# A four-layer convolution network on one core: the MLP's two halves formed together, the closing 1x1's loads issued one chunk later, the input loaded ahead of the weights

## The chip, the core and the metric

The kernel runs on one core of a Trainium2 chip. The metric is the device time of one execution in microseconds; the change is judged by the median of several executions. Before the change it is 3634.83 us (three runs, 3633.97 to 3635.65). All times within the kernel come from one profiled execution and are counted from the start of its span.

## What is computed

The input x is (3, 256, 48, 48), float32. Four layers follow each other, each of the form x = x + layer(groupnorm(x)), with 32 groups. All the edits lie in the first layer, an attention block; cut to what matters, it is this (B = 3, CC = 128, NB = 2):

```
y = silu(batchnorm(conv1x1(x, cv1_w)))          # 256 -> 256 channels
y1, y2 = y[:, :128], y[:, 128:]
outs, cur = [y1, y2], y2
for i in range(2):
    # the three batch entries serve as q, k and v of the attention
    cur = cur + attention(groupnorm1(cur), qkv_w[i], proj_w[i])
    h2 = groupnorm1(cur)
    f = gelu(conv1x1(h2, f1_w[i], f1_b[i]))     # 128 -> 256 channels
    cur = cur + conv1x1(f, f2_w[i], f2_b[i])    # 256 -> 128 channels
    outs.append(cur)
out = silu(batchnorm(conv1x1(concat(outs), cv2_w)))   # 512 -> 256 channels
```

Layer 1 is a 3x3 convolution whose weights are mixed, per batch entry, from eight expert kernels (`routing`, a sigmoid, then a weighted sum); layer 2 is a plain 3x3 convolution; layer 3 is a selective-scan block.

## The kernel before

Channels lie on the 128 partitions and the 2304 pixels along the free dimension, cut into NCH = 6 chunks of CH = 384. The engines are named as in the profile: PE multiplies, ACT (ScalarE) evaluates functions, DVE (VectorE) and POOL (GpSimd) do elementwise work, SP issues most loads, and ACT's queue issues some. Each engine takes its instructions in order, a load's issue included. The batch entries are worked on in the order 2, 1, 0 (`ORDER`).

The program goes through these stages.

1. **The start.** SP issues the small vectors (L118, L148), then the weights of layer 0 in two parts (`w0a` L375, 640 KB; `w0b` L377, 1024 KB), the attention's projection `pj` (L379, 128 KB), and then, per batch entry, x in two loads of 1152 KB, one for each 128 channels (L407). The statistics of the group norm run on DVE, one instruction for each chunk (L178) and an aggregate (L181); a chain of small steps over PE, DVE and POOL (L184 to L193, L160, L162, L410) turns them into a scale for the weights (L414) and a bias (L419 to L425). The 1x1 convolution (L431) needs all of these, and `w0a`. It has 48 PE records for a batch entry; silu (L435) reads its results. Its outputs go to DRAM (`ycat`, L439, L440), and `cur` also stays in SBUF.
2. **The first attention**, from about 100 to 724 us. Its order is written out by hand; `keep_order` ties each instruction to the one before it on its engine.
3. **The MLP between the attentions** (L805 to L823). For each batch entry and chunk `hidden` forms the 256 inner channels: for each half m, a matmul (L485) into its half of a PSUM pair, then gelu on ACT (L489). `add_back` multiplies back (L495) and DVE adds to `cur` (L499). Each chunk's `add_back` is called after the next chunk's `hidden`. The pair of PSUM comes from a pool with three buffers here (`pss`). This stage is ordered by a scheduler, which also moves work of the next attention between (`vt` L783, norms, `mlp_weights`).
4. **The second attention**, to about 1410 us.
5. **The last MLP and the closing 1x1**, from about 1410 to 1610 us, again in the written order (L882 to L930). For each batch entry six chunks of `hidden` and `add_back` are followed by six chunks of `concatenated`: sixteen PE records over the concatenated channels (L866), silu on ACT (L871), and POOL's addition of x (L876). The concatenated channels that were stored come back through `parts`, which issues two loads for a chunk on ACT's queue: `yc` (L855, 576 KB, read by PE) and `xc` (L857, 384 KB, read by POOL). Both have three buffers (`ypool`). Three chunks are loaded ahead of the loop; then, after chunk c, ACT issues the loads of the chunk three further on (L914). The pairs come from a pool with two buffers (`pss2`). Between the chunks, `aside` advances other work by a step: the norm and the routing of the batch entry finished before (L184, L193, L352, L353, L357), and the mixing of the expert kernels of batch entry 2 (48 pieces of 384 KB, `wconv`, issued by SP at L249 into six buffers; the first six are scaled on ACT at L273, the others added on DVE at L275), two steps after an MLP chunk and three after a chunk of the 1x1. After chunk 3 of batch entry 0, DVE forms the first input tile of the coming convolution (L324 to L335) and finishes the mixed weights (L256 to L261).
6. **The 3x3 convolutions** (L1348) begin at 1627.77 us, and layers 2 and 3 follow to the end of the span.

The whole network is built twice in the program; the second, a more careful attention, runs only when a flag is set, and the profile shows none of it.

Of the kernel before, what the change touches and what calls it, by code (L numbers as in the profile page):

```python
# [16 lines left out]
P = 128  # L17
B = 3
HW = 48
N = HW * HW  # L20
# [6 lines left out]
NCH = N // CH  # L27
# [42 lines left out]
W0_SPLIT = W0_AT["f1"]  # L70


ORDER = (2, 1, 0)
# [10 lines left out]
def net(  # L84
# [21 lines left out]
    nc = tc.nc  # L106
# [98 lines left out]
    def norm_stats(*args):  # L205
        return at_once(norm_steps(*args))
# [15 lines left out]
    def chunk(t, c):  # L222
        return t[:, c * CH : (c + 1) * CH]
# [136 lines left out]
    with ExitStack() as l0:  # L360
# [11 lines left out]
        mean1 = wpool.tile([P, P], F32, name="mean1")  # L372
        nc.gpsimd.memset(mean1, 1.0 / P)
        w0a = epool.tile([P, W0_SPLIT], F32, name="w0a")
        nc.sync.dma_start(w0a, w0[:, :W0_SPLIT])  # L375
        w0b = wpool.tile([P, NW0 - W0_SPLIT], F32, name="w0b")
        nc.sync.dma_start(w0b, w0[:, W0_SPLIT:])  # L377
        pj = epool.tile([P, NB, P], F32, name="pj")
        nc.sync.dma_start(pj, projw.rearrange("i p o -> p i o"))  # L379

        def w(name, at, n):
            a = W0_AT[name] + at
            if a < W0_SPLIT:
                return w0a[:, a : a + n]
            return w0b[:, a - W0_SPLIT : a - W0_SPLIT + n]
# [14 lines left out]
        with ExitStack() as p1:  # L400
            xin = p1.enter_context(tc.tile_pool(name="xin", bufs=2))
            y1p = p1.enter_context(tc.tile_pool(name="y1p", bufs=2))
            ps = p1.enter_context(tc.tile_pool(name="ps0", bufs=5, space=PSUM))
            for b in ORDER:
                xb = xin.tile([P, CT, N], F32, name="xb")
                for ct in range(CT):
                    nc.sync.dma_start(xb[:, ct, :], x[b, ct * P : (ct + 1) * P, :])  # L407
                _, gm, rstd = norm_stats([xb[:, ct, :] for ct in range(CT)], gmat, ps, "s")
                sh = small.tile([P, CT], F32, name="gsh", bufs=4)
                nc.vector.scalar_tensor_tensor(sh, gm, -1.0, rstd, ALU.mult, ALU.mult)  # L410
                ws = y1p.tile([P, CT, 256], F32, name="cv1s", bufs=2)
                pb = ps.tile([P, 512], F32, tag="s", name="ps_b1")
                for ct in range(CT):
                    nc.vector.tensor_scalar(  # L414
                        ws[:, ct, :], w("cv1", ct * 256, 256), rstd[:, ct : ct + 1], None, ALU.mult
                    )
                for m in range(2):
                    for ct in range(CT):
                        nc.tensor.matmul(  # L419
                            pb[:, m : m + 1], w("cv1", ct * 256 + m * P, P), sh[:, ct : ct + 1],  # L420
                            start=ct == 0, stop=ct == CT - 1,
                        )
                bb = small.tile([P, 2], F32, name="bb")
                nc.vector.tensor_tensor(bb, pb[:, :2], b1sc, ALU.mult)
                nc.vector.tensor_tensor(bb, bb, b1sh, ALU.add)  # L425
                y1 = y1p.tile([P, N], F32, name="y1")
                for c in range(NCH):
                    for m, dst in ((0, y1), (1, cur[b])):
                        pm = ps.tile([P, 512], F32, tag="s", name="ps_y")
                        for ct in range(CT):  # L430
                            nc.tensor.matmul(  # L431
                                pm[:, :CH], ws[:, ct, m * P : (m + 1) * P], chunk(xb[:, ct, :], c),
                                start=ct == 0, stop=ct == CT - 1,
                            )
                        nc.scalar.activation(  # L435
                            chunk(dst, c), pm[:, :CH], AF.Silu,
                            bias=bb[:, m : m + 1], scale=b1sc[:, m : m + 1],
                        )
                nc.sync.dma_start(ycat[b][:, 0, :], y1)  # L439
                nc.sync.dma_start(ycat[b][:, 1, :], cur[b])  # L440
# [6 lines left out]
        def pair():  # L447
            return pss.tile([P, 2, 512], F32, tag="s", name="ps_s")
# [31 lines left out]
        def hidden(b, c):  # L480
            wf, fb = mlp[b]
            f = fpool.tile([P, 2, CH], F32, name="f")
            pf = pair()
            for m in range(2):
                nc.tensor.matmul(  # L485
                    pf[:, m, :CH], wf[:, m * P : (m + 1) * P], chunk(cur[b], c),
                    start=True, stop=True,
                )
                nc.scalar.activation(f[:, m, :], pf[:, m, :CH], AF.Gelu, bias=fb[:, m : m + 1])  # L489
            return f  # L490

        def add_back(i, b, c, f):
            pf = psa.tile([P, 512], F32, name="acc")
            for m in range(2):
                nc.tensor.matmul(  # L495
                    pf[:, :CH], w("f2", (i * 2 + m) * P, P), f[:, m, :], start=m == 0, stop=m == 1
                )
            cc = chunk(cur[b], c)
            nc.vector.scalar_tensor_tensor(cc, pf[:, :CH], v("f2_b", i), cc, ALU.add, ALU.add)  # L499
# [352 lines left out]
        def parts(b, c):  # L852

            yc = ypool.tile([P, 3, CH], F32, name="yc")
            nc.scalar.dma_start(yc, ycat[b][:, :, c * CH : (c + 1) * CH])  # L855
            xc = ypool.tile([P, CT, CH], F32, name="xc")
            nc.scalar.dma_start(  # L857
                xc, x[b, :, c * CH : (c + 1) * CH].rearrange("(t p) n -> p t n", p=P)
            )
            return yc, xc  # L860

        def concatenated(b, c, yc, xc):
            pz = pair()
            for m in range(2):
                for kt in range(4):
                    nc.tensor.matmul(  # L866
                        pz[:, m, :CH], w("cv2", kt * 256 + m * P, P),
                        yc[:, kt, :] if kt < 3 else chunk(cur[b], c), start=kt == 0, stop=kt == 3,
                    )
            for m in range(2):  # L870
                nc.scalar.activation(  # L871
                    chunk(xs[b][:, m, :], c), pz[:, m, :CH], AF.Silu,
                    bias=b2sh[:, m : m + 1], scale=b2sc[:, m : m + 1],
                )
            both = xs[b][:, :, c * CH : (c + 1) * CH]
            nc.gpsimd.tensor_tensor(both, both, xc, ALU.add)  # L876

        def take_stats(b, c, stats):
            for m in range(2):
                nc.vector.bn_stats(stats[m][:, c, :], chunk(xs[b][:, m, :], c))  # L880

        i = NB - 1  # L882
        mark = listed[-1]
        chunks = [(b, c) for b in ORDER for c in range(NCH)]
# [4 lines left out]
        def aside(n):  # L889

            if small_steps:
                try:
                    next(small_steps[0])
                except StopIteration:
                    del small_steps[0]
            if 2 in route:
                for _ in range(n):
                    next(mixing, None)

        for n, b in enumerate(ORDER):  # L900
            held = None
            for c in range(NCH):
                f = hidden(b, c)
                if held is not None:
                    add_back(i, *held)
                held = b, c, f
                aside(2)
            add_back(i, *held)
            stats = [
                small.tile([P, NCH, 6], F32, name=f"xst{m}", bufs=2) for m in range(CT)  # L910
            ]
            for c in range(NCH):
                concatenated(b, c, *ahead.pop(0))
                z = n * NCH + c + 3  # L914
                if z < len(chunks):
                    ahead.append(parts(*chunks[z]))
                if c:
                    take_stats(b, c - 1, stats)
                if b == 0 and c == 3:
                    vp = late_pool("vp", 2, last_pools)  # L920
                    pad = late_pool("pad", stack=last_pools)
                    first_v = input_transform(2, 0, *norms[2])
                aside(3)
            take_stats(b, NCH - 1, stats)
            if b:
                curpools[b].close()
            small_steps.append(routing(b, psm, "m", stats))
# [10 lines left out]
    rooms, w3v, chunks = {}, {}, {}  # L938
# [399 lines left out]
    with ExitStack() as l1:  # L1338
# [95 lines left out]
        for n, (k, h) in enumerate(halves):  # L1434
            layer, b = units[k]
# [36 lines left out]
    with ExitStack() as l3:  # L1472
# [134 lines left out]
        for s, (at, m, h) in enumerate(steps):  # L1607
            if m == 0 and h == 1 and at + 2 <= last:
                fetch(at + 2)
            for part in range(8):  # L1610
                j = 4 * m + 2 * h + part // 4
# [150 lines left out]
```

## Time and profile before

| what | us |
|---|---|
| median of three runs | 3634.83 |
| lowest and highest | 3633.97, 3635.65 |
| the profiled execution | 3635.14 |
| its span | 3633.4 |
| busy: PE, DVE, ACT, POOL | 3195.8, 3007.2, 2338.1, 1442.2 |
| mean granted clock of PE | 0.929 of full |

The profiled execution is 1.7 us longer than its span and 0.3 us longer than the median of the runs. The page of a profile gives the busy time of each engine and, for groups of instructions, how long one takes and what the engine waited for before it. The timeline lists instructions in order of time; a line reads start, duration, engine, line of the source, operation, output <- inputs, and in brackets the idle time before it with what ended it. A 128x384 matmul in float32 shows as two PE records. "ACTq" and "SPq" mark what the queue of ACT or SP issues. A view by windows gives the busy time of each engine in stretches that one names. A wait is put down to the event that came last, so the engine named is not always the cause.

### The profile page before, as it was taken

To read this page: it belongs to the slowest core of one execution; us is meant where nothing else is said; L and a number is where in the kernel's file an instruction comes from. 1 tells how busy PE (TensorE), PEld (TensorE's weight loads), DVE (VectorE), ACT (ScalarE), POOL (GpSimd) and SP (SyncE) were. 2 spreads that over 40 slices of the span, in tenths; PEclk is the share of its full clock that TensorE was granted. 3 is DMA by queue.
4 is the path that set the end of the run, shared out by engine and by line. 5 is a ranking of instruction groups with operands and counts; after the bars stand their busy time and mean duration, and the time that the engine had idled before them with its cause. 6 is when DMAs were issued, how large, how long until landed. Compare 5 with 4: busy or idle time off the path is not lost. (4 is left out here: it accounts for less than half of the span.)

```text
span 3633.4 us, 45544 instructions
## 1 busy us (share of the span) xinstructions
PE 3195.8 (88%) x17154; PEld 1441.3 (40%) x17154; DVE 3007.2 (83%) x3304; ACT 2338.1 (64%) x3477; POOL 1442.2 (40%) x386
## 2 busy tenths in 40 slices
PE   6999999999999998867899988888888888888875
PEld 4323232342322324436677753333333333333331
DVE  3798989959989895369966469999999999999996
ACT  2688777748877875332123347777777777777774
POOL 0000000000000000210000039999999999999997
PEclk9999999999999999978899998988899999888886
DMA  4000000000000001656502134444444444444441
GB/s 171 11 1 1 1 2 1 1 39 1 2 1 1 2 1 66 198 180 220 184 15 57 46 85 103 115 109 106 107 114 96 110 101 107 111 113 101 111 105 36
DMA packets 169209, 266.50 MB, mean 73 GB/s; under 512 B 42689, under 2 KB 135937, under 8 KB 166802
## 3 DMA queue, kind: packets, MB, share of 16 engines
q1 hardware_dynamic: 150642, 243.44, 25.0%
q10 hardware_dynamic: 18336, 20.06, 1.8%
q8 instruction: 136, 2.23, 0.3%
q14 instruction: 95, 0.78, 0.1%
HBM read 216.31 MB, written 46.89 MB: 72 GB/s over the span
## 5 line engine op out<-in xcount | busy, mean ns | idle before, releaser
L603 ACT ACTIVATE pt<-ps_s 128x1024 f32<-128x1024 f32 x972 | 938.9, 1022 | 237.0 <-PE ps_s L599 219.2
L1564 DVE TENSOR_TENSOR_SCAN hs<-ps_da,hs 128x385 f32<-128x385 f32 x1152 | 1012.7, 939 | 61.1 <-ACT ps_da L1556 43.2
L679 DVE TENSOR_TENSOR part<-part,pt 128x2048 f32<-128x2048 f32 x396 | 906.7, 2290 | 80.9 <-ACT pt L603 56.4
L1556 ACT ACTIVATE ps_da<-dtr,u 128x384 f32<-128x384 f32 x1152 | 658.2, 582 | 311.0 <-DVE hs L1564 292.6
L162 POOL TENSOR_TENSOR rstd<-ve,mhalf 128x2 f32<-128x2 f32 (+1 forms) x26 | 17.9, 690 | 1564.4 <-DVE ve L160 1564.4
L599 PE MATMUL ps_s<-q,kt 32*128 32x512 f32 (+1 forms) x4320 | 616.3, 594 | 2.3 <-DVE q L560 0.9
L612 PE MATMUL acc<-pt,vt 128*32 128x512 f32 (+1 forms) x4320 | 522.9, 563 | 8.2 <-DVE o L659 8.0
L1348 PE MATMUL ps_c<-vt,u 128*128 128x288 f32 x1728 | 432.1, 412 | 44.4 <-DVE u L261 30.2
L1572 POOL TENSOR_TENSOR hc<-hs,x 128x3072 f32<-128x3072 f32 x72 | 445.9, 6193 | 36.7 <-PE ps_g L1147 13.4
L1572 POOL TENSOR_TENSOR hc<-hs,bc 128x3072 f32<-128x3072 f32 x72 | 443.8, 6165 | 37.2 <-PE ps_g L1147 13.6
L1101 PE MATMUL ps_g<-u 128*128 128x384 f32 x1152 | 388.3, 492 | 3.1 <-ACT u L1110 3.1
L1348 PEld LDWEIGHTS ps_c<-vt,u 128*128 128x128 f32 x1728 | 331.6, 193 | 139.5 <-issue 33.4
L599 PEld LDWEIGHTS ps_s<-q,kt 32*128 32x128 f32 x4320 | 220.1, 183 | 389.2 <-issue 228.5
L1101 PEld LDWEIGHTS ps_g<-u 128*128 128x128 f32 x1152 | 214.6, 190 | 174.1 <-issue 13.3
L1589 PE MATMUL ps_y<-hc,u 128*32 128x384 f32 x2304 | 247.5, 553 | 29.8 <-POOL hc L1572 26.5
L1531 POOL TENSOR_TENSOR hs<-dtur,x 128x1536 f32<-128x1536 f32 x72 | 248.3, 3449 | 16.2 <-DMA dtur<-dtud 12.8
L1531 POOL TENSOR_TENSOR hs<-dtur,bc 128x1536 f32<-128x1536 f32 x72 | 248.2, 3447 | 6.9 <-DMA dtur<-dtud 4.3
L612 PEld LDWEIGHTS acc<-pt,vt 128*32 128x32 f32 x4320 | 95.7, 108 | 365.4 <-issue 329.5
L1147 PE MATMUL ps_g<-wconv,u 17*128 17x384 f32 x144 | 79.2, 684 | 97.2 <-ACT x L1168 97.2
L1364 ACT COPY cb<-ps_c 128x288 f32<-128x288 f32 x48 | 19.1, 397 | 221.6 <-PE ps_c L1348 203.4
L1589 PEld LDWEIGHTS ps_y<-hc,u 128*32 128x32 f32 x2304 | 64.6, 118 | 200.5 <-issue 148.0
L1059 PE MATMUL ps_g<-wconv,u 128*128 128x384 f32 x144 | 86.6, 773 | 65.3 <-ACT x L1168 64.9
(236 smaller groups left out, 3548.4 us busy)
## 6 DMA issues: line engine op xcount, KB each, us to landing
wconv<-in_we SPq DMA_DIRECT2D x144, 384.0 KB, 4.3
dtr<-dtd SPq DMA_DIRECT2D x288, 192.0 KB, 3.9
dtur<-dtud SPq DMA_DIRECT2D x288, 96.0 KB, 4.1
wconv<-xd SPq DMA_DIRECT2D x36, 384.0 KB, 4.5
x<-bcd SPq DMA_DIRECT2D x72, 192.0 KB, 5.6
dtd<-x SPq DMA_DIRECT2D x36, 384.0 KB, 2.4
bc<-bcd SPq DMA_DIRECT2D x72, 192.0 KB, 5.4
yc<-ycat ACTq DMA_DIRECT2D x18, 576.0 KB, 4.9
```

Of the source, the lines that this page charges most:

```text
L599: nc.tensor.matmul(s[:, j, cols], kt[r, mt * P : (mt + 1) * P], q[r, :n], start=True, stop=True,)
L603: nc.scalar.activation(p[:, h0 : h0 + 2, :], s, AF.Exp)
L612: nc.tensor.matmul(acc[h * HD : (h + 1) * HD, :n], vt[:, mt, g * P + h * HD : g * P + (h + 1) * HD], p[:, h, cols], start=mt == 0, stop=mt ...
L679: nc.vector.tensor_tensor(part, first_p if group == 1 else part, p, ALU.add)
L1059: nc.tensor.matmul(bank[to], w3v["less"][:, int(to != ct), :], k.xg[:, ct, :], start=ct == 0, stop=ct == CT - 1,)
L1101: nc.tensor.matmul(bank[m % 2], w3v["wtap"][:, tap, ct, m * P : (m + 1) * P], k.xn[:, ct, tap : tap + CH], start=tap == 0 and ct == 0, sto ...
L1348: nc.tensor.matmul(pc[:, :HN], u[:, i, dy, ct, m * P : (m + 1) * P], vt[:, i, ct, dy * TW : dy * TW + HN], start=ct == 0 and dy == 0, stop ...
L1531: nc.gpsimd.tensor_tensor(hs[:, :, 2:4, 1:], k.rows[m][1].unsqueeze(1).broadcast_to([P, 2, 2, CH]), bb, ALU.mult,)
L1556: nc.scalar.activation(slots[n % 3][:, 1 : CH + 1], chunks[at].rows[m][0][:, q, :], AF.Exp, scale=amat[:, col : col + 1],)
L1564: nc.vector.tensor_tensor_scan(b, slots[(8 * s + part) % 3][:, : CH + 1], b, 0.0, ALU.mult, ALU.add)
L1572: nc.gpsimd.tensor_tensor(hc, tiles[s][:, :, :, 1:], cb.broadcast_to([P, 2, 4, CH]), ALU.mult)
L1589: nc.tensor.matmul(k.y_ps[32 * q : 32 * q + 32, :CH], fold, hc[:, g, q, :], start=False, stop=h == 1 and g == 1,)
```

## The change

Three edits, all in layer 0.

- In the start, the loads of x come first in SP's queue. The first batch entry's x is split into twelve loads, six for each 128 channels, of one chunk each. `w0a` is issued after them, `pj` and `w0b` after the x of the second batch entry.
- In `hidden`, both matmuls are written ahead of the two gelus. This touches the MLP between the attentions and the last MLP.
- In the closing 1x1, the loads issued after chunk c are those of the chunk two further on instead of three. Three chunks are still loaded ahead of the loop, so nothing is issued after the first chunk.

```diff
@@ layer 0, start
         w0a = epool.tile([P, W0_SPLIT], F32, name="w0a")
-        nc.sync.dma_start(w0a, w0[:, :W0_SPLIT])
         w0b = wpool.tile([P, NW0 - W0_SPLIT], F32, name="w0b")
-        nc.sync.dma_start(w0b, w0[:, W0_SPLIT:])
         pj = epool.tile([P, NB, P], F32, name="pj")
-        nc.sync.dma_start(pj, projw.rearrange("i p o -> p i o"))
...
             for b in ORDER:
                 xb = xin.tile([P, CT, N], F32, name="xb")
+
+                parts = 6 if b == ORDER[0] else 1
                 for ct in range(CT):
-                    nc.sync.dma_start(xb[:, ct, :], x[b, ct * P : (ct + 1) * P, :])
+                    for j in range(parts):
+                        at = slice(j * N // parts, (j + 1) * N // parts)
+                        nc.sync.dma_start(xb[:, ct, at], x[b, ct * P : (ct + 1) * P, at])
+                if b == ORDER[0]:
+                    nc.sync.dma_start(w0a, w0[:, :W0_SPLIT])
+                if b == ORDER[1]:
+                    nc.sync.dma_start(pj, projw.rearrange("i p o -> p i o"))
+                    nc.sync.dma_start(w0b, w0[:, W0_SPLIT:])
@@ hidden
                     start=True, stop=True,
                 )
+            for m in range(2):
                 nc.scalar.activation(f[:, m, :], pf[:, m, :CH], AF.Gelu, bias=fb[:, m : m + 1])
             return f
@@ the closing 1x1
             for c in range(NCH):
                 concatenated(b, c, *ahead.pop(0))
-                z = n * NCH + c + 3
-                if z < len(chunks):
+
+                z = n * NCH + c + 2
+                if 3 <= z < len(chunks):
                     ahead.append(parts(*chunks[z]))
```

## The prediction

> **What bounds the kernel now.** The page first, its busy times:
>
> ```profile
> PE 3195.8 (88%) x17154; PEld 1441.3 (40%) x17154; DVE 3007.2 (83%) x3304; ACT 2338.1 (64%) x3477; POOL 1442.2 (40%) x386
> ```
>
> TensorE (PE) and DVE are busy most of the span, but in different stages, and the chain that ended last names only the last 12 us, so the value of each edit is read from its own stage. I asked for busy time by stages, with borders taken from the timeline: the start up to the first convolution, the MLP between the attentions, then for batches 2, 1 and 0 the last MLP and the closing 1x1 in turn, and the wait after them. The columns are window, length, then busy us of PE, weight loads, DVE, ACT and POOL, the granted clock, the DMA engines' share, GB/s.
>
> ```profile
> 0.00:24.30 24.30, 2.90 (x13) 2.76 (x13) 10.32 (x34) 1.28 (x1) 4.11 (x17) 1.00 0.72 281
> 724.60:784.00 59.40, 58.36 (x189) 32.66 (x188) 31.84 (x79) 22.90 (x39) 1.62 (x3) 1.00 0.10 40
> 1410.30:1444.10 33.80, 22.27 (x62) 11.51 (x61) 8.85 (x27) 10.34 (x16) 0.54 (x1) 0.80 0.46 158
> 1444.10:1475.10 31.00, 31.00 (x98) 18.27 (x97) 5.72 (x11) 6.17 (x10) 9.04 (x5) 1.00 0.54 151
> 1475.10:1511.20 36.10, 23.88 (x58) 12.23 (x57) 6.26 (x22) 17.45 (x25) 2.50 (x2) 0.76 0.25 79
> 1511.20:1542.10 30.90, 30.90 (x97) 18.21 (x96) 22.43 (x26) 7.29 (x11) 10.26 (x5) 1.00 0.94 331
> 1542.10:1578.80 36.70, 25.06 (x58) 12.39 (x57) 20.21 (x37) 13.52 (x19) 2.77 (x2) 0.77 0.58 203
> 1578.80:1609.90 31.10, 31.10 (x97) 18.04 (x95) 19.57 (x25) 8.72 (x12) 11.05 (x8) 1.00 0.64 210
> ```
>
> PE is full in each 1x1 (31.0 of 31.0), and a third idle, with its clock down to 0.76 to 0.80, in each last MLP. The start is a wait for loads: engines are all but idle, the DMA engines 0.72 busy, and DVE's first statistic runs at 12.19:
>
> ```profile
> 12.19 2.86 DVE L178 BATCH_NORM_STATS2 bnst<-xb 128x6 f32<-128x384 f32 x6 [7.26 <-DMA xb<-in_x]
> ...
> 18.14 0.32 DVE L181 BATCH_NORM_AGGREGATE mv<-bnst 128x2 f32<-128x36 f32 x1
> ```
>
> The ACT and PE timelines at the border of batch 1 show why the MLP is slow:
>
> ```profile
> 1475.27 0.53 ACTq L855 DMA_DIRECT2D yc<-ycat  x1
> 1475.84 0.66 ACT L871 ACTIVATE x<-ps_s,cv2sh,cv2sc 128x384 f32<-128x384 f32 x1
> 1478.41 0.37 ACTq L857 DMA_DIRECT2D xc<-in_x  x1
> 1478.81 1.28 ACT L489 ACT_TABLE_LOAD   x1 [2.31 <-POOL x L876]
> 1480.11 0.58 ACT L489 ACTIVATE f<-ps_s,fb 128x384 f32<-128x384 f32 x1
> ```
> ```profile
> 1475.07 0.81 PE L485 MATMUL ps_s<-cur,wf 128*128 128x384 f32 x2
> 1480.74 2.92 PE L485 MATMUL ps_s<-cur,wf 128*128 128x384 f32 x4 [4.87 <-ACT f L489]
> 1484.40 1.65 PE L485 MATMUL ps_s<-cur,wf 128*128 128x384 f32 x2 [0.73 <-ACT f L489]
> 1485.84 2.77 PE L495 MATMUL acc<-f,w0b 128*128 128x384 f32 x4
> ```
>
> The xc load at L857 refills a buffer that POOL's add of this very chunk still reads; ACT issues in order, so the table load and the first gelu queue behind it. The second half's matmul waits until gelu has read the first half, though it writes other columns. After 4.9 us of idling PE works at half speed: the four records of one return product took 2.77 us (a logical matmul is two records), where at full clock the next group starts 1.29 us later (744.62 to 745.91), 0.322 a record.
>
> **What the Trainium skill says.** "TensorE: Matmul & The Clock Gate", Part 1: PE runs at half clock after an idle window of about 3.4 us until about as long a busy one. The trace agrees (2.77 against 1.29 us). "ScalarE: Activation LUTs", What ACT_TABLE_LOAD costs: about 1283 ns for a load; here 1.28. "DMA: Bandwidth & Descriptors", Issuing engines are not separate DMA queues: loads from ACT and SP share the same engines. It agrees: yc landed in 4.1 us in batch 2's 1x1, in 4.7 to 8.5 in the others, beside SP's wconv loads.
>
> **Part 1, the input ahead of the weights.** Before, w0a, w0b and pj (1792 KB) pass through SP's queue before x; the second half's aggregate ends at 18.14 + 0.32 = 18.46. Now SP issues twelve parts of 192 KB from 1.71 on, some 0.45 us each (L375 to L379). I put the first landing at 4.0 (vec: 58 KB in 1.8 us, and 0.5 for the larger size at 420 GB/s), then one part each 0.58 us, a little more than issue (0.45) or bytes (0.47), as their rows are short: the last at 10.4. One statistic (0.55) and the aggregate (0.32): 11.3, a gain of 7.2. Batch 1's statistics, two of which (0.55 each) sat between L188 and L190, now stand behind the chain: 0.3 more. From the seventh part on an issue also waits for the load eight before it (the instruction order shows it), with w0a and batch 1's x queued behind on SP; eight parts in flight are 3.7 us of bytes at 420 GB/s against 2.3 to land, so that is no brake. Together 7.5; bounds 5.5 (parts at 0.75 us) and 9.5 (paced by issue alone). What moves: w0a, behind all parts, lands near 12.3, needed at L414 about 14.9; batch 1's x lands near 17, its convolution starts near 38; vb, w0b and pj are needed after 85 us; POOL's queue is not touched. All cost nothing. The convolution of batch 2, and what follows, starts at 16.8 for 24.3.
>
> **Part 2, both halves first, between the attentions.** Period per chunk there: 2.93 us (741.69 to 744.62), work 8 records of 0.322 = 2.58. So 0.35 lost in about 10 of 18 chunks, as the others already had two halves together, and 0.5 at the start: 4. Bounds 2 and 6. Gelu of the first half now waits for both matmuls, 0.65 later: only the chunk's second gelu stands behind it, and the return product comes after the next chunk's pair, so it is hidden; without that pair between, it would cost 0.65 a chunk. Batch norms and vt keep PE busy after it.
>
> **Parts 2 and 3 in the last MLPs.** Let h be a pair of hidden matmuls (1.29), a the return product (1.29), f two gelus (1.05).
>
> Batch 2: ACT still issues three chunk loads until 1417.5, so gelu starts at 1418.85 as before; but two h are ready. PE order after: h0 h1 a0 h2 a1 ... a5. f0 is done at 1419.9; a0 and part of h2 run at half clock (PE was idle since 1413.5), to 1424.7; then eight of 1.29 and 0.8 of small products: 1436.0. Before: 1444.1. Gain 8.
>
> Batch 1, from t = 0 at h0: silus end 1.4, the loads' buffer was freed a chunk ago, table 1.45 to 2.73, f0 3.8 (before: first gelu at 5.0, a0 at 10.8). a0 3.9, then gm, h2, a1, gv, h3, a2: 10.7. The routing chain remains: L499 to sigmoid took 2.05 us, so sigmoid at 12.95; two L273 (1.76) and a table load: f4 17.3, two L273, f5 20.2, a5 21.6. Before 36.1. Gain 14.5; less 1.5, if one idle window halves the clock: 13.
>
> Batch 0: the same, but DVE does two L275 (1.94) between the steps of the norm chain, which becomes the limit: aggregate 5.5, gd 8.9, pooled 13.0, sigmoid 17.0, then h4 at half clock after 4 us of idling, table, f4, f5, a5 near 26. Before 36.7. Gain 10.7.
>
> The cost is part 3's own: yc for chunk c+2 is issued at the end of chunk c, so it must land in 5.16 - 0.2 = 5.0 us, where it had 10. Cover is one chunk of PE work. In batch 2 it lands in 4.1: free. In batches 1 and 0, with landings 4.7, 4.9, 5.3, 7.7 and about 5.5, 8.5 for the six loads that count, the excess sums to 0.3 + 2.7 + 0.5 + 3.5 = 7; a stall also slows DVE and so SP's competing loads, so I take 5, bounds 0 and 15. If xc is late it stops POOL and the statistics behind it, not PE, and it has a chunk more. The first product of a chunk reads yc, so a late load holds all of PE's queue. Lost cover would cost the whole landing, 4.1 us or more a chunk.
>
> After chunk 3 of batch 0 DVE's own chain (L324 to L261, 1603.5 to 1627.5) sets when the next convolution may start; it hangs on POOL's add of that chunk, so all of it moves. Last stage: 8 + 13 + 10.7 - 5 = 26.7, bounds 12 and 35.
>
> **The sum.** 7.5 + 4 + 26.7 = 38.2 off the profiled execution (span 3633.4 and 1.7 around it, 3635.1), which stands 0.3 above the median of 3634.8: 3597.
>
> **The rivals.** (a) The norm chain and ACT's tables fill most of the gap: for it stands that sigmoid still waits for four engines and that DVE stands in L275; against it that PE's largest waits (4.87, 5.19) go. Last stage 12: 3611. (b) The clock stays full and no yc is late: 38.2 + 5 + 1.5 + 3 (batch 0's h4): 3587. (c) The end of the stage is set by the 48 mixing steps and their 19 MB: only parts 1 and 2 count, 11.5: 3623. Against: DVE idles 4.22 us before L324, and 42 more loads of 0.39 MB with 12 chunks of 0.98 MB, 28 MB in some 89 us, need 318 GB/s, where 331 was reached. (d) Slower: the yc loads at L855, queued in the ring with six wconv loads, land so late that each of the six tight chunks stalls. It takes 43.2 us of stalls to eat the gain, 7.2 each, that is landings over 12.2; the longest seen is 8.5. At 13.5 us, 8.5 each, 51: 3643. (e) That the halves stay apart is excluded by the instruction order, in which each pair stands together with no wait between.
>
> **Chances.** Forecast 0.57 (own range 3590 to 3606), (a) 0.20, (b) 0.13, (c) 0.07, (d) 0.03. The range 3581 to 3614 takes in the forecast, (a) and (b), so 0.9 before misjudged sizes. A measurement can tell about 0.2%, 7.3 us, from no change: faster 0.96, same 0.01, slower 0.03.
>
> **What would show it.** First L178 near 4, first long convolution near 16.8; MLP period 2.6; the three last MLPs at 26, 22 and 26 us with clock above 0.8; PE waits on yc of 0 to 3 us in the 1x1 of batches 1 and 0. Yc landings over 8 us, or the wait before L1348 much above 17.9, would prove me wrong.

## The result, and the profile after

The kernel after took 3597.6 us (median of 4 runs, 3594.8 to 3598.5) beside 3635.2 for the kernel before (median of 4 runs, the three of the table above and one more): a ratio of 0.9895, 95% interval 0.9878 to 0.9913. All ratios below are likewise to the kernel before, run beside the kernel in question. The forecast was 3597. The profiled execution after spans 3596.3 us, 37.1 less than before. Lines of the code up to L374 keep their numbers; in the parts at issue they move by 6 to 8 (the hidden matmul L485 is now L491, gelu L496, return product L502, the 1x1's matmul L873, yc's load L862, xc's L864, and the first matmul of the 3x3 convolutions L1356). That matmul is the first to use the mixed weights and is called the first mixing matmul below; "the mixing starts" means its start.

The busy times by stage, in the columns of the table before (window, length, PE, weight loads, DVE, ACT, POOL, granted clock, DMA share, GB/s):

```profile
0.00:18.43 18.43, 2.88 (x13) 2.74 (x13) 8.78 (x30) 1.28 (x1) 4.11 (x17) 1.00 0.86 298
718.70:776.00 57.30, 56.72 (x193) 33.93 (x193) 32.87 (x84) 20.92 (x39) 1.62 (x3) 1.00 0.15 62
1401.55:1427.17 25.62, 19.47 (x62) 11.65 (x61) 8.85 (x27) 9.53 (x16) 0.54 (x1) 0.87 0.60 208
1427.17:1458.13 30.96, 30.96 (x97) 18.24 (x96) 5.72 (x11) 6.20 (x11) 9.04 (x5) 1.00 0.41 128
1458.13:1478.88 20.75, 17.98 (x57) 9.58 (x56) 6.26 (x22) 15.73 (x24) 2.51 (x2) 1.00 0.34 109
1478.88:1515.85 36.97, 33.14 (x97) 18.83 (x96) 20.40 (x27) 8.13 (x12) 9.69 (x5) 0.95 0.92 322
1515.85:1539.82 23.97, 19.47 (x57) 10.52 (x56) 17.66 (x36) 12.71 (x19) 2.83 (x2) 0.93 0.70 231
1539.82:1572.60 32.78, 30.86 (x96) 17.88 (x95) 17.88 (x23) 8.88 (x13) 10.06 (x8) 1.00 0.74 246
```

Read the third, fifth and seventh row, the last MLPs: 25.6, 20.75 and 24.0 us for 33.8, 36.1 and 36.7. Two things shrank. In batch 1, PE's idle time fell from 12.2 to 2.8 us, and the same matmuls took 17.98 us of PE in place of 23.88, because the clock stayed at 1.00. The sixth and eighth row show the price: two of the three 1x1s, which PE filled in 30.9 to 31.1 us, now take 37.0 and 32.8.

The border of batch 1 in the timeline, ACT and PE together:

```profile
1458.13 3.04 PE L491 MATMUL ps_s<-cur,wf 128*128 128x384 f32 x8
...
1458.96 0.57 ACTq L864 DMA_DIRECT2D xc<-in_x  x1
...
1459.67 1.28 ACT L496 ACT_TABLE_LOAD   x1
1460.96 2.00 ACT L496 ACTIVATE f<-ps_s,fb 128x384 f32<-128x384 f32 x4
...
1461.59 1.56 PE L502 MATMUL acc<-f,w0b 128*128 128x384 f32 x4 [0.42 <-ACT f L496]
```

Four halves (8 records) stand together without a wait; xc is issued 0.83 after the MLP's start where it was 3.34, as its buffer is free; the table load follows at 1.54 (before 3.74), and PE waits 0.42 us where it waited 4.87.

One of the stalls that pay for it, in batch 1's 1x1:

```profile
1495.53 0.55 ACTq L862 DMA_DIRECT2D yc<-ycat  x1
...
1503.76 3.67 PE L873 MATMUL ps_s<-yc,w0b 128*128 128x384 f32 x6 [3.17 <-DMA yc<-ycat]
```

The load issued at 1495.53 lands 8.1 us later. PE waits 3.17 us for it, and then takes 3.67 us for six records that take 2.10 at full clock.

The start, DVE and PE:

```profile
4.53 1.10 DVE L178 BATCH_NORM_STATS2 bnst<-xb 128x6 f32<-128x384 f32 x2 [1.59 <-DMA xb<-in_x]
6.70 0.56 DVE L178 BATCH_NORM_STATS2 bnst<-xb 128x6 f32<-128x384 f32 x1 [1.07 <-DMA xb<-in_x]
...
12.97 0.32 DVE L181 BATCH_NORM_AGGREGATE mv<-bnst 128x2 f32<-128x36 f32 x1
...
18.43 0.99 PE L437 MATMUL ps_y<-xb,cv1s 128*128 128x384 f32 x1
```

The first statistic runs at 4.53 in place of 12.19, and the long convolution starts at 18.43 in place of 24.27, 5.84 earlier.

Where the 37.1 us of span lie: the start 5.84; nothing up to the first MLP (700.2 us of convolution and attention for 700.3); 2.8 from there to the last stage; 26.67 between the last stage's first hidden matmul and the first mixing matmul (190.79 for 217.46); 1.66 in the two milliseconds behind it, which the change doesn't touch and which vary by up to 4.1 among the kernels below (2003.5 to 2007.6).

### The profile page after: what moved, and what is told of

Its sections match the earlier page's. It is cut to its first block, busy times and chain, and to the rows that moved or that the text cites. A ratio compares the mean times of both kernels' runs of the same rounds, so it can differ in the third digit from the quotient of the medians.

```text
span 3596.3 us, 45582 instructions
## 1 busy us (share of the span) xinstructions
PE 3179.0 (88%) x17154; PEld 1438.0 (40%) x17154; DVE 3003.0 (84%) x3304; ACT 2333.6 (65%) x3477; POOL 1440.4 (40%) x386
## 3 DMA queue, kind: packets, MB, share of 16 engines
q1 hardware_dynamic: 152082, 243.44, 25.2%
## 5 line engine op out<-in xcount | busy, mean ns | idle before, releaser
L1356 PE MATMUL ps_c<-vt,u 128*128 128x288 f32 x1728 | 430.0, 410 | 45.7 <-DVE u L261 45.7
L1356 PEld LDWEIGHTS ps_c<-vt,u 128*128 128x128 f32 x1728 | 330.3, 192 | 140.1 <-issue 34.8
```

The lines of the kernel that those rows point to most:

```text
L1356: nc.tensor.matmul(pc[:, :HN], u[:, i, dy, ct, m * P : (m + 1) * P], vt[:, i, ct, dy * TW : dy * TW + HN], start=ct == 0 and dy == 0, stop ...
```

## The experiments

Each kernel is named with its edit. The table, worked out from the timelines' first matmuls, carries most of what follows: start of the first long convolution, start of the last stage, then the lengths of MLP and 1x1 in turn (the last column of these ends with the first mixing matmul), when that matmul starts, and the median.

| kernel | conv. at | stage at | MLP 2 | 1x1 | MLP 1 | 1x1 | MLP 0 | 1x1 to mixing | mixing at | median |
|---|---|---|---|---|---|---|---|---|---|---|
| before | 24.27 | 1410.3 | 33.8 | 30.96 | 36.1 | 30.96 | 36.7 | 48.99 | 1627.8 | 3635.2 |
| after | 18.43 | 1401.6 | 25.6 | 30.96 | 20.75 | 36.97 | 24.0 | 52.51 | 1592.3 | 3597.6 |
| input alone | 18.18 | 1404.3 | 33.6 | 30.96 | 36.05 | 30.96 | 36.5 | 48.98 | 1621.4 | 3627.8 |
| halves alone | 24.44 | 1407.5 | 25.8 | 30.96 | 23.05 | 30.96 | 26.2 | 48.98 | 1593.4 | 3602.8 |
| later loads alone | 24.20 | 1411.2 | 33.9 | 30.96 | 32.8 | 36.5 | 30.2 | 51.2 | 1626.9 | 3632.4 |
| input and halves | 17.94 | 1400.5 | 25.0 | 30.96 | 22.9 | 30.96 | 29.1 | 48.98 | 1588.3 | 3594.5 |
| yc three ahead, xc two | 18.56 | 1401.3 | 25.7 | 30.96 | 20.76 | 30.96 | 26.9 | 48.98 | 1585.5 | 3587.3 |
| both one ahead | 18.67 | 1402.0 | 25.9 | 52.5 | 20.75 | 68.1 | 25.0 | 70.3 | 1664.6 | 3670.0 |
| less mixing in MLP 0 | 18.79 | 1401.0 | 25.2 | 30.96 | 20.75 | 30.96 | 25.5 | 51.8 | 1586.1 | 3590.2 |
| loads after the MLP | 17.96 | 1400.5 | 25.4 | 30.96 | 20.75 | 30.96 | 25.7 | 48.97 | 1583.2 | 3589.5 |
| both of these | 17.61 | 1399.5 | 24.9 | 30.96 | 20.76 | 30.96 | 22.1 | 51.8 | 1581.0 | 3589.9 |

Each row is one execution, and stretches with the same code do not repeat exactly, so the table also says what can be told apart. Among the eight kernels with the new start the convolution begins at 17.61 to 18.79. In all rows with the halves batch 2's MLP has the same code, and it takes 24.9 to 25.9 us (26.7 in a kernel of the last experiment). A 1x1 in which PE never waits repeats within 0.02 us. Batch 0's MLP repeats worst: the two kernels with the halves and without the later loads have the same code there and take 26.2 and 29.1. A difference of one or two microseconds in it shows nothing by itself.

### Each part alone

The first three kernels are the kernel before with one of the three parts of the change's diff each; the fourth is the kernel after without the last part. They have no diff of their own.

Input alone:

> The kernel before with the input ahead of the weights and nothing else. Theory (the start's gain is kept to the end, as every later stage begins from it): the trace of the kernel after starts the first long convolution 5.84 us earlier, so 3635.2 - 5.8 = 3629.4, bounds 3628 and 3631. Rival (a later wait for a load or for GpSimd absorbs it): 3635.

Measured: 3627.8, ratio 0.9977 (0.9969 to 0.9986). The start gained 6.1 in its trace and the mixing began 6.3 earlier, so nothing absorbs it: the rival's 3635 is out. The median lies just below the theory's bound of 3628. Its gain of 7.7 is 1.4 more than the stages account for, no more than the stretch behind the mixing varies.

Halves alone:

> The kernel before with both hidden halves formed first and nothing else. Theory (the halves alone restore most of the last MLPs; the blocked ACT costs some 2.3 us and one half-clock window in each of batches 1 and 0): 2.9 between the attentions, 8.2 in batch 2's MLP, about 11.6 in batch 1's, about 10 in batch 0's, no stall on yc: 32.7 off, 3602.5, bounds 3598 and 3608. Rival (without the later loads the MLPs of batches 1 and 0 stay near 33 us, as ScalarE's late table load is what lets TensorE fall to half clock): 2.9 + 8.2 + 6, 3618.

Measured: 3602.8, ratio 0.9913 (0.9899 to 0.9926). The theory's 3602.5 holds, and 3618 is out. The one added line in `hidden` brings the mixing's start 34.4 us forward: 2.8 between the attentions, 8.0, 13.0 and 10.5 in the three last MLPs, where 2.9, 8.2, 11.6 and 10 were forecast. The blocked table load is still there, and costs little:

```profile
1467.57 0.38 ACTq L858 DMA_DIRECT2D xc<-in_x  x1
...
1468.03 1.28 ACT L490 ACT_TABLE_LOAD   x1 [2.37 <-POOL x L877]
```

xc is issued when POOL's add has ended, 3.35 us into the MLP, the table load waits 2.37 us for that, and batch 1's MLP is 2.3 longer than in the kernel after.

Later loads alone:

> The kernel before with the last 1x1 loads one chunk later and nothing else. Theory (the earlier gelu leaves TensorE idle for 2.6 us instead of 4.9, so that it may keep its clock, and the 1x1 loses about 8 to late yc): MLPs of batches 1 and 0 shorter by 6 to 9 each, so 3635.2 - 15 + 8 + 1 = 3629, bounds 3625 and 3640. Rival (only together with the halves: split halves keep TensorE at half clock): MLPs 2.3 shorter each, 1x1 8 longer, 3638.

Measured: 3632.4, ratio 0.9987 (0.9978 to 0.9995), between the two theories and nearer to the first's 3629. The MLPs of batches 1 and 0 gain 3.3 and 6.5, the two 1x1s lose 5.6 and 2.2, and the mixing starts 0.9 earlier. The first theory's reason, that a pause of 2.6 us lets TensorE keep its clock, holds in one MLP and fails in the other. In batch 1 the pause was 2.57 us and half clock followed at once; in batch 0 it was 2.66 us and the clock stayed full until the routing, 16 us later. Over the whole MLPs the clock was 0.79 and 0.89. The windows that tell the two pauses apart stand in the last section.

Input and halves, the later loads left out:

> The kernel after with the last 1x1 loads put back, issued three chunks ahead. Theory (in company of the other two parts the later loads give about what their stalls take: some 3.7 us in batch 1's MLP and 2.7 in batch 0's against 6.0 and 2 in the 1x1): 3597, within 4 of the kernel after's 3597.6. Rival (the later loads carry the MLPs' gain): 3612. Other rival (the stalls are worse than the blocked ScalarE): 3590 or less.

Measured: 3594.5, ratio 0.9889 (0.9874 to 0.9904), beside 0.9878 to 0.9913 for the kernel after: they can't be told apart, as the first theory had it. By the stages, the later loads give 2.2 in batch 1's MLP and 5.1 in batch 0's, and take 6.0 and 3.5 behind them: 2.3 lost. With the halves alone batch 0's MLP took 26.2 and not 29.1; against that the loads give it only 2.2, and more is lost. The code of the two is the same there, but one had two windows of 3.41 us at half clock in it and the other four. The third part of the change is worth nothing on its own balance; the first two carry it all (7.7 and 32.7 alone, 41.0 together).

### What the later loads cost, and how to keep their gain

Both loads one chunk ahead, the cover taken away wholly:

```diff
-                z = n * NCH + c + 2
+                z = n * NCH + c + 1
```

> The kernel after with the last 1x1 loads one chunk ahead in place of two: the suspected cost, cover of yc, is taken away wholly for 13 of 18 chunks. Theory (TensorE then stalls in each for the whole landing, 4.1 us in batch 2 and about 5.5 in the others, and computes the next products at half clock, 2.2 more): 3 x 6.3 + 10 x 7.7 less the 9.5 already paid, so about 87 later, 3684, bounds 3655 and 3700. Rival (a stall only gives the mixing on DVE time that it needs anyway, so the end of the stage hardly moves): 3610 or less.

Measured: 3670.0, ratio 1.0095 (1.0079 to 1.0112). The mixing starts 72 later than in the kernel after, where 87 was expected. What waited for yc, and the time from issue to landing, from the view of that tile:

```profile
  DMA yc<-ycat: 75.3, 15
...
DMA to landing us min/median/max: 4.2/4.4/5.9
```

Thirteen of these waits are of PE's matmuls, 4.4 to 6.1 us each, 62 in all. In batch 2's 1x1 three stalls cost 21.5 and in batch 1's five cost 37.1, on average 7.2 and 7.4 each: the stall, and some 2.5 us for products at half clock behind it. In batch 0 five stalls cost only 21.3, three times 7.1. The missing 14 us are the two stalls behind chunk 3, hidden beside DVE's chain to the mixing, as the prediction read that stage: from ScalarE's instruction that opens this chain (L310) to the mixing 25.7 us passed here, and 27.2 in the kernel after, which has no stall there. The rival, that stalls cost next to nothing, is out.

yc three chunks ahead as before the change, xc two as after it, in place of `parts`, which loads both:

```diff
+                z = n * NCH + c + 3
+                if z < len(chunks):
+                    ahead.append(part_y(*chunks[z]))
+                if 3 <= z - 1 < len(chunks):
+                    ahead_x.append(part_x(*chunks[z - 1]))
```

> The kernel after with the two last 1x1 loads taken apart: yc three chunks ahead as before the change, xc two chunks ahead as after it. Theory (only xc's buffer blocks ScalarE, as GpSimd's add still reads it, and only yc's short cover stalls TensorE): MLPs stay at 20.8 and 24.0 us, batch 1's 1x1 returns to 30.96 (6.0 off) and batch 0's stretch to the mixing to 49.0 (3.5 off): 3597.6 - 9.5 = 3588, bounds 3585 and 3591. Rival (the stalls are the transfers' bandwidth, not their issue time): 3597. Rival (xc with two chunks' cover holds GpSimd's add and through it the routing): 3593.

Measured: 3587.3, ratio 0.9867 (0.9851 to 0.9884), the lowest median here; its runs (3585.4 to 3590.8) all lie below those of the kernel after. From the view of yc's tile:

```profile
L875 PE MATMUL ps_s<-yc,w0b x216: 486/486/486, 1427.0 to 1566.5; 128*128 128x384 f32 x108
...
DMA to landing us min/median/max: 4.1/6.0/9.9
```

All 216 matmuls that read yc take the same 486 ns, and none waits, though the landings became longer (median 6.0, in the kernel after 4.7). So the transfers' bandwidth was not the stall; their issue time was. The other rival, that xc comes late for POOL, is out too. All 18 additions waited for ScalarE's silu and none for xc; what their engine waited for, from the view of xc's tile:

```profile
  ACT x L880: 98.9, 18
```

yc's buffer is freed by PE's own read of the chunk and blocks nobody; only xc's, which POOL's add still reads, held ScalarE. Both 1x1s return to 30.96 and 48.98. But batch 0's MLP took 26.9, not 24.0. The table load came 4.8 us after its start, where it came 1.6 in the kernel after:

```profile
1512.50 0.53 ACTq L861 DMA_DIRECT2D yc<-ycat  x1
1514.01 0.40 ACTq L866 DMA_DIRECT2D xc<-in_x  x1
1514.52 1.28 ACT L496 ACT_TABLE_LOAD   x1 [3.40 <-DVE u L275]
```

The silus ended at 1511.13, and yc's issue stood until 1512.50, xc's until 1514.01, with the table load behind both; xc's buffer was free. A semaphore is the counter that tells of a load's landing. In the trace this yc load has the semaphore of the wconv load that SP issued at 1505.45 and that landed at 1512.48, and this xc load that of the wconv load of 1506.38, which landed at 1513.95. Each issue came within 0.06 us of that landing: ScalarE waited for transfers of another queue that had been under way for 7.0 and 7.6 us.

Two edits on top of that kernel. Less mixing in batch 0's MLP, more behind it:

```diff
-                aside(2)
+                aside(2 if b else 1)
...
-                aside(3)
+                aside(3 if b else 4)
```

> The kernel with yc three chunks ahead and xc two (3587.3), with one mixing step in place of two per chunk of batch 0's last MLP, and four in place of three per chunk of the 1x1 behind it. Theory (DVE's L275 between the steps of the norm chain is what makes batch 0's MLP longer than batch 1's 20.8): the chain has three pairs of L275 in it, 0.97 off each, so the MLP falls from 26.9 to about 24, the 1x1 has room for one more step a chunk (4 x 0.95 + 1.0 = 4.8 of 5.16 us), total 3584.4. Rival (the MLP waits for ScalarE's blocked loads, not for DVE): MLP 26.5, 3587. Other rival (the moved steps come late behind the 1x1): 3590.

The two loads that stand ahead of the table load issued after the MLP:

```diff
+            if n:
+                load(n * NCH + 2)
...
+                if c < NCH - 1:
+                    load(n * NCH + c + 3)
```

> The kernel with yc three chunks ahead and xc two (3587.3), with the two loads that stand between a batch's last silu and the next MLP's first gelu issued after that MLP instead. Theory (in batch 0 the yc issue waited at 1512.5 on ScalarE for a wconv load of SP's with the same semaphore, and xc at 1514.0 for another, and table load and gelus were queued behind): batch 0's first gelu 3 us earlier, its MLP near 24, batch 1's unchanged at 20.8, 3584.3. Rival (the norm chain with its L275 sets batch 0's MLP anyway): 26 to 27, 3587. Other rival (the loads come later for the 1x1, and TensorE stalls there): 3590 or more.

And both:

> Both of these edits together. Theory (both mechanisms are at work and independent): batch 0's MLP near 21 to 22, 3581.5. Rival (either alone already frees the same path): 3584.

Measured: 3590.2, 3589.5 and 3589.9, ratios 0.9877 (0.9860 to 0.9893), 0.9875 (0.9858 to 0.9891) and 0.9877 (0.9861 to 0.9894). None of the totals can be told from 3587.3, so none of the forecasts of 3581.5 to 3584.4 is borne out, and what follows is from one trace of each kernel. Loads after the MLP: the table load came 1.5 us after the MLP's start (before this edit 4.8), yet the MLP shortened by only 1.2 of the expected 2.9. The next long wait, the routing's, remains; its matmul in that kernel:

```profile
1523.88 0.59 PE L353 MATMUL ps_r<-rwt,pbc 128*128 128x8 f32 x2 [3.54 <-DVE pbc L352]
```

It waits for DVE's norm chain with its pairs of L275. Thinning them alone took 1.4 off, both edits 4.8. That fits two limits beside each other, each of which hides part of what the other gives, but it is not shown: 1.2 and 1.4 lie within what this MLP varies with the same code, and with both edits it also had one window at half clock in place of two. The mixing steps moved into the 1x1 returned 2.8 us there, as the second rival had it: from L310 to the mixing 29.8 us pass in both kernels with them, and 27.0 without.

### The start

Two parts a half, and three:

```diff
-                parts = 6 if b == ORDER[0] else 1
+                parts = 2 if b == ORDER[0] else 1
```

> The kernel after with batch 2's input in two parts a half (four loads of 576 KB) in place of six. Only the start is read from its trace: the first long convolution stands at 18.43. Theory (short rows and many issues slow the loads: the engines moved 180 to 230 GB/s from 4.2 to 6 us): the first statistic comes later, near 6, but the last part lands near 9.5 with three statistics behind it, so the convolution is 1 to 1.5 earlier, 17.1. Rival (the rate is set by the chip's first transfers, whatever their rows, and the last part has three statistics behind it): 18.4 to 19.5. No change of the total beyond 1.5 us in either.

> The kernel after with batch 2's input in three parts a half (six loads of 384 KB, rows of 3072 bytes). Read from its start alone. Theory (row length and issues set the pace): the last part lands near 9.8, two statistics follow, convolution near 16.9. Rival (pace independent of the rows): 18.4 to 19.

Measured, one execution each: convolution at 17.79 and 18.51, totals 3600.4 and 3599.8. The forecasts of 17.1 and 16.9 are missed, and neither kernel can be told from those with six parts, whose convolution starts at 17.61 to 18.79.

With two parts the DMA engines moved 378 GB/s from 4 to 6 us, where six parts moved 223. But the first statistic ran only at 5.67, and the last part landed at 10.19, where about 9.5 was forecast. From 9.16 to the aggregate at 12.33 DVE worked without a pause; the aggregate ended 2.46 us behind the last landing, where three statistics and an aggregate alone would need 1.97. With three parts the rate was 361 GB/s from 4 to 6 us, but 227 from 6 to 8, where six parts moved 336. The third part landed at 8.31, DVE waited 1.16 us for it, and the last landed at 11.60, where 9.8 was forecast.

So longer rows did not bring the last part in as early as the theory had it, and DVE can make up little of a late landing: its twelve statistics of 0.55 and two aggregates of 0.32 are 7.24 us, whatever the parts. What sets the pace of the first loads stays open.

## Why the prediction was right, step by step

**The whole.** 38.2 off was forecast, 37.1 of span came, 37.6 by the medians. The last stage's 26.7 came as 26.67. That closeness is luck. The three last MLPs gave 36.2 where 31.7 was forecast, and the yc loads took 9.5 where 5 was: two errors of 4.5 that cancelled. The start and the stretch between the attentions fell 2.8 short together, and 1.7 came from the stretch behind the mixing, which the change does not touch.

**The start, 7.5: measured 5.84** (5.5 to 6.7 among the kernels with this start). The term that was off is the landings: "I put the first landing at 4.0", "then one part each 0.58 us", "the last at 10.4". By the trace the parts landed at 4.50, 5.04, 6.68 and 7.80, and from there on every 0.53 us, the last at 12.08. So the pace held from the fourth part on, and what was missing is the first landing's 0.5 and the late third and fourth part. DVE's work behind the first landing is 7.24 us without any wait, as much as the 7.3 that the prediction had between 4.0 and 11.3, so it could make up nothing: a first statistic at 4.53, 7.24 of work and two waits for the third and fourth part (1.07 and 0.56) make 13.40, and the aggregate ended at 13.29. From there to the convolution 5.14 us passed, where 5.5 was reckoned. Why the third and fourth part came late was not tried.

**Between the attentions, 4: measured 2.8.** The period fell to 2.58 as said (734.16, 736.74 and 739.32 are return products in a row), and the start gained 0.52 for 0.5. But ten chunks were counted as losing 0.35 each, and in four of these a norm's small product already stood in the gap: there the period fell only from 2.93 to 2.81. Six times 0.35, four times 0.12 and the 0.52 make 3.1.

**Last MLPs.** Batch 2: 8 forecast, 8.2 measured. Batch 1: 13 forecast, 15.35 measured; sigmoid came at 12.85 of the 12.95 worked out, and the deduction of 1.5 for one window of half clock was not needed: the clock stayed at 1.00. Batch 0: 10.7 forecast, 12.7 measured; norm chain and sigmoid ran as listed, each a microsecond sooner (sigmoid at 15.9 for 17.0), and h4 at half clock. One reading on the way was loose: 2.77 us at half clock is the length of a return product, and 1.29 is the distance to the next group; the same product's length at full clock is 1.45 (L495 at 744.62).

**The yc loads, 5 within 0 and 15: measured 9.5.** The waits were three, 0.66, 3.17 and 1.92 us, 5.75 in all, so the size of the stalls themselves was right. Two terms were missing. A stall also halves the clock: in batch 1, 6.0 were lost for 3.8 of waiting. And in batch 0 the last chunk's loads moved past the instruction that opens DVE's chain:

```profile
1563.45 1.69 ACTq L864 DMA_DIRECT2D xc<-in_x  x1
...
1565.18 1.39 ACT L310 ACTIVATE xpad<-x,six 128x1200 f32<-128x1200 f32 x1 [1.13 <-issue]
```

Before, no load was left to issue in chunk 3, and this instruction ran 22.0 us into the 1x1; now it runs at 25.4, of which 2.1 is PE's stall and 1.1 this issue. The prediction asked of SP's queue what the moved loads pass there, and not of ScalarE's.

**The reason given for part 3** holds in its mechanism and not in its weight. The table load did queue behind xc's issue, and that goes; but the halves alone remove most of the gap, and what part 3 adds (2.2 and 5.1 us) its stalls take back. The prediction priced both parts as one sum, so it could not see that.

**The rivals.** (a), a gap filled by norm chain and tables, is out at 26.67, though in batch 0 that chain is what remains. (b) came true in part: full clock in batch 1, but late loads. (c), the mixing as the end of the stage, is out: the first product behind it came 35.4 us earlier, with everything ahead of it. (d) needed 43 us of stalls; with one chunk of cover less it happens, at 3670. Two of the signs were set too tight: yc landings of 8.1 and 9.2 us were seen, over the 8 named, and the first cost 3.2 us; and the wait before the first mixing matmul rose from 17.86 to 19.23, by ScalarE's late start of the chain.

## What to carry to other kernels

When two loads are issued together, ask of each separately who frees its buffer and who waits for it: here one needed the early issue and the other the free buffer, and moving them as a pair made the gain and the loss cancel. Where a wait makes TensorE idle, look for what stands between products that write different columns of one tile; lifting it cost one line and gave most of the result. Price a stall of TensorE with the half-clock time behind it, and price each part of a change alone before summing.

## What the runs showed of the hardware

The clock halves without an idle window. The Trainium skill, "TensorE: Matmul & The Clock Gate", Part 1, has the half clock begin after an idle window of about 3.4 us, on a grid of its own. The grid is in the records here: spells of half clock last 3.41 us or multiples of it. But the window that brings them need not be idle. From the kernel with the later loads alone, two windows of the grid that stand ahead of a spell of half clock, each followed by the first window of that spell (window, length, PE, weight loads, DVE, ACT, POOL, clock, DMA share, GB/s):

```profile
1476.43:1479.84 3.41, 0.84 (x3) 0.30 (x2) 0.37 (x1) 2.99 (x4) 1.80 (x1) 1.00 0.59 168
1479.84:1483.25 3.41, 2.68 (x5) 1.06 (x4) 1.04 (x4) 1.16 (x2) 0.00 (x0) 0.50 0.32 120
1493.50:1496.91 3.41, 2.13 (x10) 1.11 (x8) 1.10 (x3) 1.89 (x4) 0.00 (x0) 1.00 0.00 0
1496.91:1500.32 3.41, 0.75 (x2) 0.00 (x0) 0.00 (x0) 3.38 (x4) 0.00 (x0) 0.50 0.42 121
```

PE was busy for 0.84 and 2.13 of 3.41 us, and its longest pause was 2.57 and 0.90. Nor does a pause of that length always bring the half clock. In batch 0 of the same kernel the grid cuts the pause of 2.66 us, which ends at 1548.96, in two; neither window is emptied, and the clock stays full:

```profile
1544.69:1548.11 3.42, 1.61 (x5) 0.60 (x4) 2.79 (x4) 2.31 (x3) 1.10 (x1) 1.00 0.62 188
1548.11:1551.52 3.41, 1.83 (x5) 0.95 (x6) 2.35 (x6) 1.95 (x4) 1.03 (x1) 1.00 1.04 391
```

The busy share alone does not decide every case: in the kernel with input and halves a window with the same 2.13 us of work (1467.65 to 1471.06) kept the clock. All thirteen traces together, from 30 us on, show a band. Of the windows at full clock, all 376 in which PE was busy for less than 0.40 of the time were followed by half clock, and none of the 10,797 with more than 0.65; between these, 118 lost the clock and 437 kept it. So in these kernels a pause cost the clock by how much of a single window it took, and that depends on where it fell on the grid. That is also how the same code can have two or four windows at half clock in batch 0's MLP.

ScalarE's queue can be held by a load of SP's: two issues stood for 1.4 and 1.0 us, up to 1512.50 and 1514.01, with their own buffers free; by the semaphores they waited for wconv loads that had been under way for over 7 us, and they came 0.02 and 0.06 us behind those landings. That the table load runs at 1.5 us once the two loads are moved from this place fits, but the wait itself was not tried alone.
